# Two chunks of a depthwise convolution on ScalarE and GpSimd, one chunk fewer on TensorE, and the skip term on GpSimd

## The chip, the cores and the metric

The kernel runs on one core of one Trainium2 chip. Its time is the device time of one execution in microseconds (us), from the first to the last instruction on that core. A core has five engines that run side by side, each with its own queue in a fixed order: TensorE (PE), VectorE (DVE), ScalarE (ACT), GpSimd (POOL) and SyncE (SP, which here only issues DMAs). An instruction that waits holds up everything behind it on its own engine.

## The reference, cut to what matters

Two layers of a visual state-space block run one after the other over an image of 64 x 64 positions with 96 channels. In each layer an input projection gives 192 channels `x_val` and 192 gates `z`; `x_val` goes through a depthwise 3 x 3 convolution, a bias and SiLU. The result `u` feeds four selective scans, and the skip term `u * D` is added to their sum.

```python
xz = x @ in_proj_w                       # (H, W, 96) -> (H, W, 384)
x_val, z = (xz[..., :D_INNER], xz[..., D_INNER:])
xc = conv_general_dilated(xc, conv_w, (1, 1), 'SAME', feature_group_count=D_INNER) + conv_b
x_val = silu(xc)                         # u
y = scans(u) + u * D_skip                # four directions, summed
y = layernorm(y) * silu(z)
x = x + y @ out_proj_w
```

The convolution has nine taps; for each channel it is a sum of nine products of a shifted image with one weight of that channel.

## The kernel before, in words

`two_ss2d_layers` runs `head` (group norm, projections, convolution, gates), then the scans (`near_scans` in layer 0, `scans` in layer 1), then `tail`, once per layer. The change touches `head` alone, so it acts twice in an execution: at about 20 to 82 us (layer 0) and 205 to 271 us (layer 1).

The 192 channels lie as three blocks of 64 channels on 64 partitions; the two halves of each group of rows sit on partitions 0 to 63 and 64 to 127. A block has four chunks of 8 rows each per half, so a chunk is a tile of 128 partitions x 512 elements. Each block's projected image lies in SBUF with a border of zeros, `pad[b]` (128 x 4 chunks x 10 rows x 66 columns); `project` (line 1171) and `borders` (line 1183) fill it by TensorE and copies on ScalarE (lines 1179 and 1197).

There are two ways to convolve:

- `conv` (line 1237) runs on VectorE: one product with a weight (line 1251) and eight multiply-adds into an accumulator (line 1253). Over two chunks at once the operand is 2 x 526 = 1052 elements a partition, and both the image and the accumulator lie in SBUF. The accumulator comes from a pool with three buffers (tag `acc`).
- `conv_by_products` (line 1224) runs on TensorE: nine matmuls of one chunk with a diagonal matrix of the weights (line 1228), summed in PSUM.

Both end in `finish` (line 1217): ScalarE applies the bias and SiLU and writes `u` (line 1218), and `start_y` (line 1127) writes `y = D u` (line 1128), also on ScalarE.

The head's work, from line 1256 on: VectorE convolves block 0 (two pairs of chunks), block 1 (two pairs) and the last chunk of block 2; TensorE makes the first three chunks of block 2. The twelve gate chunks follow (`gate`, line 1201): a matmul (line 1205), SiLU on ScalarE (line 1210) and a DMA to HBM through three buffers (line 1211). The head isn't ordered by hand: the scheduler that records the program orders each engine's queue by its own estimates. On VectorE it lays two pairs of chunks into each other, a step of one and a step of the other by turns. The scans of layer 1 are in a hand-written order. GpSimd has almost nothing to do in the head: it clears the borders of `pad`.

After the head of layer 0, `near_scans` first copies parts of `u` by matmuls (`nu`, lines 283 to 299), in the order block 0, 1, 2. After the head of layer 1, `scans` first projects the last chunk of `u`, blocks 0, 1, 2 (`pj`, shown by the profile as line 675, since all its instructions are recorded by one helper).

Of the kernel before, what the change touches and what calls it, by code (L numbers as in the profile page):

```python
# [8 lines left out]
F32 = mybir.dt.float32  # L9
# [7 lines left out]
HW = 64  # L17
# [7 lines left out]
HT = TC // 2  # L25
NCH = L // TC
SR = HT // HW
# [9 lines left out]
V_CW, V_CB, V_G, V_B, V_D = 0, 9, 10, 11, 12  # L37
# [6 lines left out]
def two_ss2d_layers(  # L44
# [29 lines left out]
    nc = tc.nc  # L74
# [78 lines left out]
    with tc.tile_pool(name="ld", bufs=8) as ld, tc.tile_pool(  # L153
        name="ldp", bufs=4, space=PSUM
# [972 lines left out]
    def start_y(mul, ds, T, s=slice(0, L // 2)):  # L1127
        mul(y[T][:, s], u[T][:, s], ds[:, T : T + 1])

    def head(l, xT, w):  # L1130

        ipw_s, v, ds = w["ipw"], w["v"], w["ds"]
        with ExitStack() as sc:
            cv = sc.enter_context(tc.tile_pool(name=f"cv{l}", bufs=1))
            cw = sc.enter_context(tc.tile_pool(name=f"cw{l}", bufs=3))
            cvp = sc.enter_context(tc.tile_pool(name=f"cvp{l}", bufs=2, space=PSUM))

            pad = [cv.tile([128, NCH, SR + 2, HW + 2], F32, name=f"pad{l}_{b}") for b in range(3)]
# [24 lines left out]
            for g in range(8):  # L1163
                s = slice(g * 512, (g + 1) * 512)
# [6 lines left out]
            def project(b, c):  # L1171
                ps = cvp.tile([128, HT], F32, tag="in", name=f"in{l}_{b}_{c}", bufs=3)
                for h, half in enumerate(HALF):
                    g = 2 * c + h
                    nc.tensor.matmul(  # L1175
                        ps[half], ipw_s[:, 64 * b : 64 * b + 64], xn[:, g * 512 : (g + 1) * 512],
                        start=True, stop=True,
                    )
                nc.scalar.copy(
                    pad[b][:, c, 1 : SR + 1, 1 : HW + 1], ps.rearrange("p (r w) -> p r w", w=HW)  # L1180
                )

            def borders(b):

                ps = cvp.tile([128, 2, NCH, HW], F32, tag="ed", name=f"ed{l}_{b}")
                lhs = ipw_s[:, 64 * b : 64 * b + 64]
                for h, half in enumerate(HALF):
                    for below in range(2):

                        row = [SR * (2 * c + h + below) - 1 + below for c in range(NCH)]  # L1190
                        cs = [c for c in range(NCH) if 0 <= row[c] < HW]
                        s = slice(cs[0], cs[-1] + 1)
                        nc.tensor.matmul(
                            ps[half, below, s], lhs, xr[:, row[cs[0]] : row[cs[-1]] + 1 : 2 * SR],
                            start=True, stop=True,
                        )
                        nc.scalar.copy(
                            pad[b][half, s, (SR + 1) * below, 1 : HW + 1], ps[half, below, s]
                        )
# [13 lines left out]
            taps = [(i, j) for i in range(3) for j in range(3)]  # L1213

            W2 = HW + 2

            def finish(b, cut, of):
                nc.scalar.activation(
                    u[b][:, cut].rearrange("p (c r w) -> p c r w", r=SR, w=HW), of, AF.Silu,
                    bias=v[:, b, V_CB : V_CB + 1],  # L1220
                )
                start_y(nc.scalar.mul, ds, b, cut)

            def conv_by_products(b, c):

                ps = cvp.tile([128, HT], F32, tag="in", name=f"cp{l}_{b}_{c}", bufs=3)
                for k, (i, j) in enumerate(taps):
                    nc.tensor.matmul(  # L1228
                        ps.rearrange("p (r w) -> p r w", w=HW), diag[:, k, :],
                        pad[b][:, c, i : i + SR, j : j + HW],  # L1230
                        start=(k == 0), stop=(k == len(taps) - 1),
                    )
                finish(
                    b, slice(HT * c, HT * (c + 1)), ps.rearrange("p (c r w) -> p c r w", c=1, w=HW)
                )

            def conv(b, s):


                n = s.stop - s.start  # L1240
                room = cw.tile([128, 2, SR, W2], F32, tag="acc", name=f"acc{l}_{b}_{s.start}")
                room = room[:, 0:n]
                acc = room.rearrange("p c r w -> p c (r w)")[:, :, 0 : SR * W2 - 2]
                for k, (i, j) in enumerate(taps):
                    o = i * W2 + j
                    src = pad[b].rearrange("p c r w -> p c (r w)")[
                        :, s, o : o + SR * W2 - 2
                    ]
                    wk = v[:, b, V_CW + k : V_CW + k + 1]
                    if k == 0:  # L1250
                        nc.vector.tensor_scalar_mul(acc, src, wk)
                    else:
                        nc.vector.scalar_tensor_tensor(acc, src, wk, acc, ALU.mult, ALU.add)  # L1253
                finish(b, slice(HT * s.start, HT * s.stop), room[:, :, :, 0:HW])

            for b in (0, 1, 2):
                project(b, 0)
                project(b, 1)
                borders(b)
            for b in (2, 0, 1):  # L1260
                project(b, 2)
                project(b, 3)
            diag = cv.tile([128, len(taps), 128], F32, name=f"diag{l}")
            for k in range(len(taps)):
                nc.scalar.mul(diag[:, k, :], ident, v[:, 2, V_CW + k : V_CW + k + 1])
            conv(0, slice(0, 2))
            for c in range(NCH - 1):
                conv_by_products(2, c)
            for b, c in ((1, 0), (0, 2), (1, 2)):
                conv(b, slice(c, c + 2))  # L1270
            conv(2, slice(NCH - 1, NCH))
            for b in range(3):
                for c in range(NCH):
                    gate(b, c)
# [85 lines left out]
    for l in range(2):  # L1360

        w = {"st": st[l], "next": st[1]}
        ipw_s = w["ipw"] = wts.tile([DM, 2 * DI], F32, name=f"ipw{l}")
        nc.sync.dma_start(out=ipw_s, in_=ipw[l])
        v = w["v"] = wts.tile([128, 3, NV], F32, name=f"v{l}")
        op = w["op"] = wts.tile([128, 3, DM], F32, name=f"op{l}")
        for half in HALF:
            nc.sync.dma_start(out=v[half], in_=vec[l].rearrange("(b p) n -> p b n", b=3))
        for half in HALF:
            nc.sync.dma_start(out=op[half], in_=opw[l].rearrange("(b p) n -> p b n", b=3))  # L1370
        ds = w["ds"] = wts.tile([128, 3], F32, name=f"ds{l}")
        nc.vector.reduce_sum(ds, v[:, :, V_D : V_D + 4], axis=AX.X)
        sw = scan_weights(l)

        head(l, xT, w)
        xp.close()
        if l:
            scans(sw)
        else:
            covered = near_scans(sw)  # L1380
            with tc.If(covered < 1):
                for T in range(3):
                    start_y(nc.scalar.mul, ds, T)
                far_scans(sw)
        xp = ExitStack()
        xT = xp.enter_context(tc.tile_pool(name=f"xT{l + 1}", bufs=1)).tile(
            [DM, L], F32, name=f"xT{l + 1}"
        )
        tail(l, w, xT)
# [80 lines left out]
```

## Time and profile before

Times of three executions: 1526.31, 1535.46 and 1537.91 us, median 1535.46. The profiled execution is another one, with a span of 1528.7 us; that span is its own time, and every duration below is from it.

| stretch of the profiled execution | length | VectorE busy | ScalarE busy | TensorE busy | GpSimd busy |
|---|---|---|---|---|---|
| 30 to 80 us, convolution and gates of layer 0 | 50.0 | 48.5 | 29.0 | 45.9 | 0.0 |
| 80 to 125 us, start of the near scans | 45.0 | 27.6 | 28.7 | 15.2 | 18.2 |
| 221 to 271 us, convolution and gates of layer 1 | 50.0 | 49.1 | 28.8 | 45.9 | 0.0 |
| 300 to 1480 us, scans of layer 1 | 1180.0 | 1120.8 | 1036.3 | 987.1 | 1063.6 |

A line of the timeline gives the start in us from the start of the span, the time from the first start to the last end in us, the engine, the line of code, the operation, the output and inputs by tile name, the shape, and the number of instructions; in brackets how long the engine had stood idle before, and what ended that. A group's line gives busy us and mean ns of one.

### The profile page before, as it was taken

What the parts mean: (1) busy time and instruction counts of PE and PEld (TensorE: products, weight loads), DVE (VectorE), ACT (ScalarE), POOL (GpSimd) and SP (SyncE); (2) the same over time, 40 slices, a digit from 0 to 9 for tenths busy, and PEclk for the clock granted to TensorE, in tenths of its full rate; (3) what the DMA queues carried; (4) which work ended last, traced back from release to release, by engine and by line L of the source; (5) the groups of instructions that cost most, each with busy time, mean ns of one, the idle gap of its engine ahead of it and who ended that gap; (6) DMA issues with size and microseconds to landing.
All of it is one profiled execution on the core that took longest, in us unless ns stands there. A gap on an engine that the chain in (4) does not pass through costs nothing.

```text
span 1528.7 us, 17324 instructions
## 1 busy us (share of the span) xinstructions
PE 1238.4 (81%) x5122; PEld 499.9 (33%) x5122; DVE 1358.4 (89%) x946; ACT 1209.9 (79%) x2475; POOL 1103.3 (72%) x593
## 2 busy tenths in 40 slices
PE   6935779788887888888798889797888797877777
PEld 3323433333232333333332333333333232322223
DVE  5957579579999999999999999999999999999976
ACT  6554255679898989898998999989898998988733
POOL 0032000369899898989898989898999999898850
PEclk9965789589899999999999999999989999999999
DMA  4230511514352626262626262635344352626232
GB/s 111 79 85 2 134 44 69 140 29 111 85 130 65 148 61 153 55 140 56 140 57 138 57 144 70 142 75 127 91 104 109 87 128 68 150 59 152 55 105 75
DMA packets 79604, 146.33 MB, mean 96 GB/s; under 512 B 27484, under 2 KB 30748, under 8 KB 79404
## 3 DMA queue, kind: packets, MB, share of 16 engines
q1 hardware_dynamic: 78348, 142.78, 38.6%
q0 software_dynamic: 576, 1.57, 0.5%
q8 instruction: 42, 0.69, 0.2%
q10 hardware_dynamic: 576, 0.79, 0.2%
q14 instruction: 62, 0.51, 0.1%
HBM read 80.85 MB, written 12.13 MB: 61 GB/s over the span
## 4 chain that ended last, share of the span: by engine, by line
DVE 27%; issue 22%; PE 15%; ACT 10%; POOL 5%; DMA 5%; SPq 4%; DVEq 0%; ACTq 0%; POOLq 0%
DVE h L675 17%; DVE b L675 7%; PE ys L675 4%; ACT a L675 4%; SPq L675 4%; POOL hc L675 4%; PE b L675 3%; PE pj L675 3%; DMA cb<-C 2%; ACT bT L675 2%; PE pd L675 2%; PE cp L1228 2%; DMA szt<-szd 1%; DVE w L675 1%; PE in L1175 1%
## 5 line engine op out<-in xcount | busy, mean ns | idle before, releaser
L675 POOL TENSOR_TENSOR hc<-h,cb 128x1024 f32<-128x1024 f32 x384 | 903.3, 2369 | 115.1 <-DVE h L675 56.2
L675 DVE TENSOR_TENSOR_SCAN h<-a,carry,b 128x1024 f32<-128x1024 f32 x288 | 665.2, 2337 | 29.9 <-PE b L675 8.7
L675 ACT ACTIVATE a<-dt,am 128x1024 f32<-128x1024 f32 x384 | 438.8, 1143 | 93.5 <-DVE h L675 90.2
L675 PE MATMUL ys<-hc,fold 128*64 128x512 f32 x1536 | 431.9, 642 | 1.9 <-POOL hc L675 1.9
L675 ACT ACTIVATE bT<-duT,BT 128x192 f32<-128x192 f32 x1012 | 387.7, 446 | 9.9 <-PE b L675 8.0
L675 PE MATMUL b<-ident,bT 128*128 128x128 f32 x1536 | 219.5, 287 | 33.9 <-DVE h L675 28.3
L675 DVE TENSOR_TENSOR b<-b,du 128x1024 f32<-128x1024 f32 x192 | 232.2, 1209 | 12.4 <-PE b L675 12.4
L675 DVE TENSOR_TENSOR_SCAN h<-a,b 128x1024 f32<-128x1024 f32 x96 | 216.2, 2278 | 13.2 <-PE b L675 5.2
L675 PEld LDWEIGHTS b<-ident,bT 128*128 128x128 f32 x1536 | 174.1, 146 | 160.6 <-DVE h L675 98.9
L675 PE MATMUL b<-B,selh 96*128 96x512 bf16 x384 | 121.6, 400 | 92.2 <-DVE h L675 92.0
L675 PEld LDWEIGHTS ys<-hc,fold 128*64 128x64 f32 x1536 | 78.7, 139 | 140.4 <-issue 96.5
L675 PE MATMUL pj<-u,xw 64*124 64x512 f32 x192 | 98.4, 662 | 4.8 <-ACT sz L1210 3.5
L675 PE MATMUL pd<-xd,dwb 29*64 29x512 f32 x192 | 59.7, 698 | 52.3 <-DVE w L675 45.5
L675 PEld LDWEIGHTS <-selh 96*128 96x128 bf16 x384 | 25.9, 98 | 221.9 <-DVE h L675 123.8
L1253 DVE SCALAR_TENSOR_TENSOR acc<-pad,v,acc 128x1052 f32<-128x1052 f32 (+1 forms) x80 | 91.3, 1198 | 0.7
L675 POOL DMA_DIRECT2D du<-su x12 | 6.4, 538 | 80.4 <-ACT am L233 78.4
L675 PE MATMUL ys<-y,ident 128*128 128x512 f32 (+1 forms) x120 | 64.2, 643 | 0.0
L675 ACT CAST B<-pj 96x512 bf16<-96x512 f32 (+2 forms) x96 | 54.9, 575 | 4.4 <-PE pj L675 4.4
L675 POOL TENSOR_TENSOR sp<-sp,ln 128x512 f32<-128x512 f32 x45 | 57.6, 1279 | 0.2
L675 POOL TENSOR_TENSOR ln<-ln,w 128x512 f32<-128x512 f32 x45 | 57.6, 1280 | 0.0
L675 POOL TENSOR_TENSOR su<-sp,u 128x512 f32<-128x512 f32 x45 | 57.5, 1278 | 0.0
L675 PEld LDWEIGHTS pj<-u,xw 64*124 64x124 f32 x192 | 35.2, 198 | 65.0 <-issue 45.5
(175 smaller groups left out, 1185.1 us busy)
## 6 DMA issues: line engine op xcount, KB each, us to landing
cb<-C SPq DMA_DIRECT2D x256, 256.0 KB
dt<-sp SPq DMA_DIRECT2D x192, 128.0 KB
du<-su SPq DMA_DIRECT2D x180, 128.0 KB
szd<-sz SPq DMA_DIRECT2D x24, 256.0 KB
szt<-szd SPq DMA_DIRECT2D x24, 256.0 KB
xT<-xs SPq DMA_DIRECT2D x8, 384.0 KB
xs<-xT SPq DMA_DIRECT2D x1, 1536.0 KB
xs<-xT SPq DMA_DIRECT2D x8, 192.0 KB
```

Of the source, the lines that this page charges most:

```text
L675: return lambda *args, **more: tc.keep_in_program_order(op(*args, **more))
L1175: nc.tensor.matmul(ps[half], ipw_s[:, 64 * b : 64 * b + 64], xn[:, g * 512 : (g + 1) * 512], start=True, stop=True,)
L1228: nc.tensor.matmul(ps.rearrange("p (r w) -> p r w", w=HW), diag[:, k, :], pad[b][:, c, i : i + SR, j : j + HW], start=(k == 0), stop=(k == ...
L1253: nc.vector.scalar_tensor_tensor(acc, src, wk, acc, ALU.mult, ALU.add)
```

## The change

Four edits, all in `head`:

1. A new function `conv_by_two` convolves two chunks without VectorE. ScalarE makes nine products of the shifted image with a weight (the first into the accumulator, the others into one of two buffers, tag `tap`), and GpSimd adds the eight others to the accumulator one after the other. It is called for chunks 2 and 3 of block 1.
2. TensorE convolves two chunks of block 2 instead of three, and VectorE the last two instead of the last one. VectorE thus has four pairs of chunks, and no single chunk.
3. `y = D u` is written by GpSimd, not ScalarE.
4. Chunks 2 and 3 of the blocks are projected in the order 1, 0, 2, not 2, 0, 1.

```diff
-                start_y(nc.scalar.mul, ds, b, cut)
+                start_y(nc.gpsimd.tensor_scalar_mul, ds, b, cut)
...
+            def conv_by_two(b, s):
+
+                n = s.stop - s.start
+                room = cw.tile([128, 2, SR, W2], F32, tag="accp", name=f"acc{l}_{b}_{s.start}", bufs=1)
+                room = room[:, 0:n]
+                acc = room.rearrange("p c r w -> p c (r w)")[:, :, 0 : SR * W2 - 2]
+                for k, (i, j) in enumerate(taps):
+                    o = i * W2 + j
+                    src = pad[b].rearrange("p c r w -> p c (r w)")[
+                        :, s, o : o + SR * W2 - 2
+                    ]
+                    wk = v[:, b, V_CW + k : V_CW + k + 1]
+                    if k == 0:
+                        nc.scalar.mul(acc, src, wk)
+                        continue
+                    part = cw.tile(
+                        [128, 2, SR, W2], F32, tag="tap", name=f"tap{l}_{b}_{s.start}_{k}", bufs=2
+                    )[:, 0:n].rearrange("p c r w -> p c (r w)")[:, :, 0 : SR * W2 - 2]
+                    nc.scalar.mul(part, src, wk)
+                    nc.gpsimd.tensor_add(acc, acc, part)
+                finish(b, slice(HT * s.start, HT * s.stop), room[:, :, :, 0:HW])
...
-            for b in (2, 0, 1):
+            for b in (1, 0, 2):
                 project(b, 2)
                 project(b, 3)
...
             conv(0, slice(0, 2))
-            for c in range(NCH - 1):
+            conv_by_two(1, slice(2, NCH))
+            for c in range(NCH - 2):
                 conv_by_products(2, c)
-            for b, c in ((1, 0), (0, 2), (1, 2)):
-                conv(b, slice(c, c + 2))
-            conv(2, slice(NCH - 1, NCH))
+            for b, s in ((1, slice(0, 2)), (0, slice(2, NCH)), (2, slice(2, NCH))):
+                conv(b, s)
```

## The prediction

> **What bounds the kernel now.** First the page, for the span and what GpSimd's operations cost:
>
> ```profile
> span 1528.7 us, 17324 instructions
> ...
> L675 POOL TENSOR_TENSOR hc<-h,cb 128x1024 f32<-128x1024 f32 x384 | 903.3, 2369 | 115.1 <-DVE h L675 56.2
> ...
> L675 POOL TENSOR_TENSOR su<-sp,u 128x512 f32<-128x512 f32 x45 | 57.5, 1278 | 0.0
> ```
>
> Two-input GpSimd operations cost 2369 ns at 1024 elements and 1278 at 512: 2.13 ns an element plus 0.19 us. Then VectorE's timeline over the convolution of layer 0:
>
> ```profile
> 29.96 0.77 DVE L1251 TENSOR_SCALAR acc<-pad,v 128x1052 f32<-128x1052 f32 x1 [7.60 <-ACT pad L1197]
> ...
> 32.68 17.23 DVE L1253 SCALAR_TENSOR_TENSOR acc<-pad,v,acc 128x1052 f32<-128x1052 f32 x14
> 49.83 0.76 DVE L1251 TENSOR_SCALAR acc<-pad,v 128x1052 f32<-128x1052 f32 x1
> ...
> 52.95 0.76 DVE L1251 TENSOR_SCALAR acc<-pad,v 128x1052 f32<-128x1052 f32 x1
> 53.63 17.23 DVE L1253 SCALAR_TENSOR_TENSOR acc<-pad,v,acc 128x1052 f32<-128x1052 f32 x14
> 70.78 0.49 DVE L1251 TENSOR_SCALAR acc<-pad,v 128x526 f32<-128x526 f32 x1
> ...
> 73.21 5.65 DVE L1253 SCALAR_TENSOR_TENSOR acc<-pad,v,acc 128x526 f32<-128x526 f32 x7
> ```
>
> No idle time from 29.96 to 78.86: VectorE sets the length of this stage, 48.9 us, and again in layer 1 (221.25 to 270.14). A multiply-add of a pair takes 17.23 / 14 = 1.23 us, its product 0.68, a pair 0.68 + 8 x 1.23 = 10.5; the single chunk 0.41 + 8 x 0.81 = 6.9. What follows waits a little earlier, in layer 1 on TensorE's timeline:
>
> ```profile
> 268.43 8.07 PE L675 MATMUL pj<-u,xw 64*124 64x512 f32 x12 [3.49 <-ACT sz L1210]
> ```
>
> `pj` starts 1.7 us before VectorE ends, when the last gate leaves ScalarE; block 2 is needed only by its third matmul. In layer 0 the copies `nu` likewise run from 76.90 to 84.75, block 2 last.
>
> Last, do VectorE and GpSimd disturb each other? In the convolution GpSimd is idle, so I look where both work, at the start of the near scans; GpSimd first, then VectorE:
>
> ```profile
> 95.94 1.23 POOL L335 CAST nB<-nleft 32x768 bf16<-32x768 f32 x1
> 101.33 3.77 POOL L370 TENSOR_TENSOR ndu<-nv,nus 64x1152 f32<-64x1152 f32 x1 [4.16 <-DVE nv L361]
> ```
>
> ```profile
> 96.60 1.79 DVE L359 TENSOR_TENSOR nw<-nw,nt 128x1152 f32<-128x1152 f32 x1
> ...
> 99.89 1.36 DVE L361 TENSOR_TENSOR nv<-nv,nln 128x1152 f32<-128x1152 f32 x1
> 101.29 1.35 DVE L370 TENSOR_TENSOR ndu<-nv,nus 64x1152 f32<-64x1152 f32 x1
> 102.67 4.85 DVE L372 TENSOR_TENSOR_SCAN nsums<-steady,nv 128x1152 f32<-128x1152 f32 x1
> ```
>
> They take turns. L359 takes 1.79 us and L361, of the same form, 1.36: L359 ends 1.22 us after GpSimd's cast does (97.17). GpSimd's L370 should take 0.19 + 1152 x 2.13 = 2.64 and takes 3.77: it ends (105.10) 2.46 after VectorE's L370 (102.64). The scan L372, some 2.6 us by the shorter scans, takes 4.85: it ends (107.52) 2.42 after GpSimd's L370. All three VectorE operations have two inputs in SBUF.
>
> **What the Trainium skill says.** "SBUF — State Buffer", section "Who interferes with whom": a VectorE instruction with two SBUF inputs shares a read path with a GpSimd instruction that reads SBUF, and the one that comes second "fully blocks" until the other ends; so does a VectorE operation with one source in a two-port mode. The three pairs above agree. It also says one SBUF input on VectorE does no harm: in the scans, where `b` lies in PSUM, GpSimd's products keep to 2369 ns. "GPSIMD Engine Reference", section "Engine selection": one-input GpSimd operations run roughly at line rate, two-input ones about twice as slow as on VectorE. The trace has the second (2369 ns against 1.36 us at 1152); for the first, a cast of 768 elements takes 0.82 us, 0.82 ns an element beside a fixed 0.19.
>
> **The change part by part**, in layer 0 (layer 1 has the same order on every engine).
>
> *Removed from VectorE:* the single chunk, 6.9. Its four pairs are 42.0 us: alone they would end at 72.0, not 78.86.
>
> *Added on GpSimd:* eight additions of 1052 elements, 0.19 + 1052 x 2.13 = 2.43 us each, 19.4 in all. Each reads two tiles of SBUF while VectorE runs multiply-adds, which read two tiles of SBUF (`pad`, `acc`). By the turns above each addition stops VectorE for as long as it holds the path: between 2.25 (2.43 less the 0.18 by which 2.46 falls short of 2.64, spent before it needs the path) and 2.43. I take 2.3: 8 x 2.3 = 18.4. If the lock did not hold here it would be 0, the lower bound (additions elsewhere can't make a multiply-add shorter); against 0 speak only the three pairs.
>
> *Who wins the path hardly matters.* By turns, an addition and a multiply-add take 3.45 us together; the first starts at 41.3 (its operand comes from ScalarE at 40.1), the eighth ends at 67.8. If VectorE always won, the additions would run later, when VectorE waits for a buffer (below), at the same total.
>
> *Added on ScalarE:* nine products of about 1.17 us (row `y<-u,ds`, 1.15 at 1024), 10.5, minus seven or eight `y` writes, 7.4. With two `tap` buffers product k waits for addition k-2, so ScalarE's queue stands in the taps until addition 6 ends (60.9). Behind it stand the SiLU table load, `u` of block 1, then `u` of chunks 0 and 1 of block 0, which frees the `acc` buffer VectorE's fourth pair needs; then the gates. By turns: addition 8 at 67.8, `u` 69.0, buffer free at 70.2; VectorE reaches that pair at 72.4, because it was held up itself. No stall, slack 2.2. The gates run from 72.4 to about 85 (before, twelve took 13.2 with interruptions), free some 6 us before VectorE's last `u`. Hence nothing on the path. Their twelve DMAs on SP's queue move with them, by about 9 us; SP's next work, the rows `nC` of the near scans (before, at 88.08) or `C` of the scans, comes after VectorE's end and moves further. If VectorE ended before 86, the gates would set the end instead.
>
> *TensorE:* nine matmuls fewer, 23.45 / 3 = 7.8 us, hidden: TensorE then waits for gates, and VectorE ends later.
>
> *`y` on GpSimd:* sizes 512, 1024, 1024, 1024, 512 fall while VectorE still convolves. No row has this operation on long tiles. Low: line rate, 0.43 and 0.85 of the path, 3.4 in all; high: 1.9 cycles an element at 1.2 GHz ("GPSIMD Engine Reference", "Performance pitfalls for Q7 kernels", an estimate), 6.5. I take 3.9, near the cast's rate. Two more `y` writes come as VectorE ends; `pj` and `nu` don't wait for them, nor does the memset behind them, needed 6 us later.
>
> *Order of projections:* block 1 first costs nothing; the first pairs need chunks 0 and 1 only.
>
> *What follows:* the last SiLU is 1.15 instead of 0.72. But block 0's last pair ends 2.5 us before block 2's. Layer 0: after `u` of block 2 (VectorE's end + 1.25) only that block's last `nu` matmuls remain, 2.1 us: + 3.4, before + 5.9, gain 2.5. Layer 1: `pj` begins when `u` of block 0 is there, 1.3 before VectorE's end instead of 1.7: loss 0.4.
>
> *Sum:* VectorE ends at 78.86 - 6.9 + 18.4 + 3.9 = 94.3, i.e. + 15.4. Layer 0: + 15.4 - 2.5 = + 12.9; layer 1: + 15.4 + 0.4 = + 15.8. Together + 28.7: 1528.7 becomes 1557.4. The median of the runs lies 6.8 above the span, so **1564 us**, 1.9% slower. The case's own range: 17.4 to 19.4 for the additions, 3.4 to 6.5 for `y`, 2 us a layer for handing over: + 24 to + 42, 1555 to 1582 beside noise of some 5 each way.
>
> **The rivals.** *No lock, but the buffer (same).* VectorE isn't held up and reaches the fourth pair at 52.95. Additions of 2.49 with their gaps end at 60.1, the buffer comes at 62.4: VectorE stalls 9.5 us and ends at 81.7, + 2.9. Layers + 0.4 and + 3.3: 1539. For: no trace shows this very multiply-add beside GpSimd. Against: the two other forms with two SBUF inputs were both held.
>
> *Faster.* Neither lock nor stall: VectorE ends at 72.0, layers - 9.3 and - 6.4: 1520. This needs, besides no lock, the eighth addition before 50.7, so additions under 1.3 us each; the row says 2.4. Almost excluded.
>
> *Slower still.* One-input `y` at the high price, and VectorE waiting also for the buffer, if additions come late: 5 to 10 us a layer more, 1575 to 1585.
>
> **How the numbers follow.** Lock as worked out 0.75 (1555 to 1575), slower still 0.15, no lock 0.08, faster 0.02. Range 1547 to 1583. Within 1% (about what a measurement of this kernel tells from no change, 1520 to 1551) lies the second case; slower by over 1% lie the first and third: 0.90.
>
> **What would show it.** Right: multiply-adds while GpSimd adds show about 3.5 us instead of 1.31, eight in each layer; VectorE ends near 94 in layer 0; additions show more than 2.43, since they wait too. Wrong: 1.31 throughout and a gap of VectorE ahead of the fourth pair, ended by ScalarE, would be the second case; a gap besides the long multiply-adds the third.

## The result, and the profile after

The changed kernel takes 1569.06 us (median of four executions, 1563.4 to 1574.8) against 1535.55 of the kernel before (four, 1526.31 to 1537.91): a ratio of 1.0244, 95% interval 1.0215 to 1.0272. (The ratios here and below are those on record; they aren't the quotients of the printed medians.) It is slower, and the time lies 5 us from the 1564 predicted. The way there is not the one predicted as likeliest.

From the page of the changed kernel, the span and the rows of the new additions and of VectorE's multiply-adds (busy us and mean ns; idle time before, and what ended it):

```profile
span 1570.4 us, 17283 instructions
...
L1256 POOL TENSOR_TENSOR acc<-acc,tap 128x1052 f32<-128x1052 f32 x16 | 64.1, 4008 | 47.0 <-ACT tap L1255 45.9
...
L1275 DVE SCALAR_TENSOR_TENSOR acc<-pad,v,acc 128x1052 f32<-128x1052 f32 x64 | 83.6, 1375 | 0.1
```

An addition takes 4008 ns in the mean where 2430 were worked out; a multiply-add 1375, hardly more than the 1.31 us of one that nothing holds up. The mean hides the shape of it. All additions of the changed kernel by their line (min, median and max duration in ns):

```profile
L1256 POOL TENSOR_TENSOR acc<-acc,tap x16: 2402/2408/15221, 41.7 to 280.6; 128x1052 f32<-128x1052 f32 x16
```

Sixteen additions, eight a layer: the median is 2408, and one of 15.2 us makes the mean. VectorE's, GpSimd's and ScalarE's timelines in layer 0 say which one:

```profile
34.30 17.24 DVE L1275 SCALAR_TENSOR_TENSOR acc<-pad,v,acc 128x1052 f32<-128x1052 f32 x14
51.45 0.77 DVE L1273 TENSOR_SCALAR acc<-pad,v 128x1052 f32<-128x1052 f32 x1
52.13 2.54 DVE L1275 SCALAR_TENSOR_TENSOR acc<-pad,v,acc 128x1052 f32<-128x1052 f32 x2
76.65 0.87 DVE L1273 TENSOR_SCALAR acc<-pad,v 128x1052 f32<-128x1052 f32 x1 [21.99 <-ACT u L1218]
77.44 19.45 DVE L1275 SCALAR_TENSOR_TENSOR acc<-pad,v,acc 128x1052 f32<-128x1052 f32 x14
```

```profile
41.72 32.61 POOL L1256 TENSOR_TENSOR acc<-acc,tap 128x1052 f32<-128x1052 f32 x8 [23.00 <-ACT tap L1255]
74.30 12.56 POOL L1128 TENSOR_SCALAR y<-u,ds 128x512 f32<-128x512 f32 x5
```

```profile
41.93 1.18 ACT L1255 ACTIVATE tap<-pad,v 128x1052 f32<-128x1052 f32 x1
56.96 1.17 ACT L1255 ACTIVATE tap<-pad,v 128x1052 f32<-128x1052 f32 x1 [13.85 <-POOL acc L1256]
...
74.36 3.23 ACT L1218 ACTIVATE u<-acc,v 128x1024 f32<-128x1024 f32 x3 [1.80 <-POOL acc L1256]
```

GpSimd's first addition starts at 41.72 and gets nowhere until VectorE stops at 54.67: 41.72 + 15.22 = 56.94. VectorE's fourteen multiply-adds before that take 17.24 us, as before (17.23). They alternate between the accumulators of two pairs, start every 1.23 us and take 1.31, so each starts 0.08 us before the last has ended. The product at 51.45, which has only one input that is a tile, is laid into this chain in the same way (it starts 0.09 before the last has ended) and doesn't let the addition in either. ScalarE stands in the taps behind the addition (13.85 us), so `u` of block 0, which frees VectorE's third accumulator, comes only at 75.5 to 76.6; VectorE, whose fourth pair needs it, stands 21.99 us, and in that time the eight additions run. The `y` behind them come later than that and are still not kept out: GpSimd is at work when VectorE starts again at 76.65, and the five take 12.56 us in a row (11.7 by their medians, below), while fourteen multiply-adds take 19.45 us instead of 17.24. Layer 1 is the same, 21.99 again.

In what follows I compare heads. Head 0 runs from VectorE's first product of the convolution to ScalarE's copy into `nxd`; head 1 from the first product to VectorE's first `wl` of the scans. All starts are read from the timelines.

| kernel (its label below) | VectorE, first product to last multiply-add, layer 0 | head 0 | head 1 | both, against before | span |
|---|---|---|---|---|---|
| before | 48.90 | 57.03 | 60.58 | | 1528.7 |
| changed | 66.65 | 73.47 | 77.10 | +33.0 | 1570.4 |
| acc4 | 44.27 | 86.51 | 90.45 | +59.4 | 1588.3 |
| gaps4 | 65.12 | 72.92 | 77.29 | +32.6 | 1560.3 |
| no_sums | 42.98 | 58.80 | 55.11 | -3.7 | 1529.8 |
| no_sums_ys | 42.25 | 47.66 | 53.45 | -16.5 | 1512.4 |
| y_scalar | 64.32 | 72.06 | 78.09 | +32.5 | 1565.9 |
| y_gpsimd_only | 50.67 | 62.14 | 62.36 | +6.9 | 1539.5 |
| psum_before | 68.06 | 78.38 | 80.52 | +41.3 | 1573.1 |
| psum_acc | 60.34 | 72.15 | 73.24 | +27.8 | 1564.8 |
| gates_between | 48.90 | 53.87 | 60.59 | -3.2 | 1526.0 |
| relief_gates | 47.39 | 53.55 | 58.93 | -5.1 | 1530.7 |
| mixed_gates | 45.44 | 55.52 | 54.32 | -7.8 | 1528.2 |
| mixed_gates_fs | 51.30 | 57.90 | 63.63 | +3.9 | 1526.8 |

The span less both heads is 1411.1 us before and 1419.8 after, and 1405.3 to 1419.8 over these fourteen profiles. So of the 41.7 us between the two profiles 33.0 are the heads, which is also about the difference of the medians (33.5); the other 8.7 can't be told from what one execution differs from the next.

### The profile page after: what moved, and what is told of

It is laid out like the page before. It is cut to its first block, busy times and chain, and to the rows that moved or that the text cites. A ratio compares the mean times of both kernels' runs of the same rounds, so it can differ in the third digit from the quotient of the medians.

```text
span 1570.4 us, 17283 instructions
## 1 busy us (share of the span) xinstructions
PE 1233.6 (79%) x5086; PEld 494.5 (31%) x5086; DVE 1350.9 (86%) x928; ACT 1216.1 (77%) x2475; POOL 1206.8 (77%) x623
## 3 DMA queue, kind: packets, MB, share of 16 engines
q0 software_dynamic: 576, 1.57, 0.4%
## 4 chain that ended last, share of the span: by engine, by line
DVE 28%; issue 21%; PE 15%; ACT 11%; POOL 5%; DMA 4%; SPq 4%; DVEq 0%; ACTq 0%; POOLq 0%
DVE h L675 16%; DVE b L675 7%; PE ys L675 5%; ACT a L675 4%; SPq L675 4%; PE b L675 3%; PE pj L675 3%; ACT bT L675 2%; DMA cb<-C 2%; POOL acc L1256 2%; POOL hc L675 2%; PE pd L675 2%; DVE acc L1275 1%; DVE w L675 1%; DMA dt<-sp 1%
## 5 line engine op out<-in xcount | busy, mean ns | idle before, releaser
L1256 POOL TENSOR_TENSOR acc<-acc,tap 128x1052 f32<-128x1052 f32 x16 | 64.1, 4008 | 47.0 <-ACT tap L1255 45.9
L1275 DVE SCALAR_TENSOR_TENSOR acc<-pad,v,acc 128x1052 f32<-128x1052 f32 x64 | 83.6, 1375 | 0.1
L1205 PE MATMUL z<-xn,ipw 96*64 96x512 f32 x96 | 27.9, 690 | 40.2 <-ACT sz L1210 40.2
```

The costliest lines, as they stand in the source:

```text
L1205: nc.tensor.matmul(ps[half], ipw_s[:, DI + 64 * b : DI + 64 * b + 64], xn[:, g * 512 : (g + 1) * 512], start=True, stop=True,)
L1256: nc.gpsimd.tensor_add(acc, acc, part)
```

## The experiments

Theory A, formed on the trace after: a chain of VectorE instructions with two inputs in SBUF, each starting before the last has ended, keeps a waiting GpSimd instruction out for as long as it lasts. Theory B, the prediction's: the engines take turns. Theory C: no shared path, only the buffer. Each ratio below is against further executions of the kernel before, with medians of 1530.9 to 1531.81 us.

**acc4**: four accumulators, so that VectorE never waits for one.

```diff
-                room = cw.tile([128, 2, SR, W2], F32, tag="acc", name=f"acc{l}_{b}_{s.start}")
+                room = cw.tile([128, 2, SR, W2], F32, tag="acc", name=f"acc{l}_{b}_{s.start}", bufs=4)
```

> The changed kernel with four acc buffers on VectorE instead of three, so that its fourth pair waits for no buffer. Theory A (a chain of two-input VectorE instructions with no gap between them keeps GpSimd out of SBUF for as long as it lasts): multiply-adds stay at 1.31 us, VectorE runs from 31.6 to about 73.6 in layer 0 without a stall; the first addition waits until then, some 31 us, and the eight end near 94 (73.6 + 8 x 2.49). ScalarE, behind them, then has four u and twelve gates left and ends its part near 107 instead of 99.4: each head some 7 to 9 us longer than with the change, profiled span near 1586. Theory B (the two engines take turns): multiply-adds beside an addition 3.5 us, VectorE ends near 94 to 96, additions end near 70, heads 3 to 5 us shorter, span near 1562. Theory C (no shared path, only the buffer): additions of 2.4 us from 41.7 to 62, VectorE ends near 74, gates near 84, heads 15 us shorter, span near 1540.

Measured: 1591.18 us, ratio 1.0421 (1.0368 to 1.0474). VectorE's timeline at the end of its chain, and the additions by their line:

```profile
55.62 17.23 DVE L1275 SCALAR_TENSOR_TENSOR acc<-pad,v,acc 128x1052 f32<-128x1052 f32 x14
72.77 0.16 DVE L1394 TENSOR_REDUCE ds<-v 128x3 f32<-128x12 f32 x1
72.89 3.33 DVE L1275 SCALAR_TENSOR_TENSOR acc<-pad,v,acc 128x1052 f32<-128x1052 f32 x1
```

```profile
L1256 POOL TENSOR_TENSOR acc<-acc,tap x16: 2402/2405/33047, 42.1 to 313.4; 128x1052 f32<-128x1052 f32 x16
```

With the stall gone the kernel is slower still, by 26.4 us in the heads: the first addition now lasts 33.0 us instead of 15.2. Less the 2.4 us that it takes alone, it gets in near 72.7, at the end of the last multiply-add but one; the one left then waits for it, 3.33 us. VectorE runs a reduction of 0.16 us there (72.77), but that isn't what lets the addition in: in layer 1 the chain holds no reduction, and the first addition ends its wait at the same place (it starts at 264.54, lasts 33.05 and so gets in near 295.2). VectorE there:

```profile
294.02 1.30 DVE L1275 SCALAR_TENSOR_TENSOR acc<-pad,v,acc 128x1052 f32<-128x1052 f32 x1
295.37 3.33 DVE L1275 SCALAR_TENSOR_TENSOR acc<-pad,v,acc 128x1052 f32<-128x1052 f32 x1
```

These are the last two steps of the fourth pair. The third pair is done, so for the first time since the addition came two multiply-adds in a row go into one accumulator, and the second starts about 0.04 us after the first has ended, not 0.08 before. Nothing else of VectorE's lies there, so the gap is what is left to let the addition in; no run changes it alone. This place also says what makes the chain unbroken: two pairs laid into each other. B and C are out: a free buffer should have helped under both.

**gaps4**: acc4, and after every multiply-add VectorE clears one unused element.

```diff
                         nc.vector.scalar_tensor_tensor(acc, src, wk, acc, ALU.mult, ALU.add)
+                        nc.vector.memset(room[:, 0, 0, HW : HW + 1], 0.0)
```

> As acc4, and after every multiply-add VectorE overwrites one unused element of its accumulator (a memset of one element per partition, in a padding column that nothing uses), so that every one to three multiply-adds VectorE leaves SBUF's read path alone for some 0.06 us; 32 such in a layer, 2 us. Theory A (only a chain without a gap keeps GpSimd out): GpSimd gets in at the first gap, near 42 us; from there an addition and one or two multiply-adds by turns, eight multiply-adds of about 3.5 us, VectorE ends near 73.6 + 2 + 18.4 = 94, or 96 with y; additions end near 72; span about 1564, some 20 us below acc4. Theory A' (VectorE has priority whenever both want the path, gap or not): no addition before VectorE ends near 76, span as acc4 plus 4. Theory B (turns anyway): no difference to acc4 but the 2 us of memsets in each layer. Theory C: 1.31 us throughout, span near 1544.

Measured: 1564.27 us, ratio 1.0226 (1.0188 to 1.0264). VectorE's timeline between 45 and 52 us, then the additions:

```profile
45.15 3.45 DVE L1275 SCALAR_TENSOR_TENSOR acc<-pad,v,acc 128x1052 f32<-128x1052 f32 x1
45.17 0.06 DVE L1276 MEMSET acc<- 128x1 f32 x1
48.52 3.46 DVE L1275 SCALAR_TENSOR_TENSOR acc<-pad,v,acc 128x1052 f32<-128x1052 f32 x1
```

```profile
L1256 POOL TENSOR_TENSOR acc<-acc,tap x16: 3292/3302/3357, 40.8 to 273.5; 128x1052 f32<-128x1052 f32 x16
```

More work on VectorE, and 27 us faster than acc4 (28.0 between the spans). A memset of 0.06 us between multiply-adds is enough: no addition waits longer than one multiply-add (3302 - 2408 = 0.9 us), and a multiply-add beside one takes 3.45 us. This is the prediction's picture, by turns, with its number; it is just not what an unbroken chain did. It also ends where the changed kernel ends: the heads are 0.4 us apart.

**no_sums** and **no_sums_ys**: the additions left out, with `y` on GpSimd and on ScalarE.

```diff
-                    nc.gpsimd.tensor_add(acc, acc, part)
```

```diff
-                start_y(nc.gpsimd.tensor_scalar_mul, ds, b, cut)
+                start_y(nc.scalar.mul, ds, b, cut)
```

> The changed kernel without its eight additions on GpSimd: eight of the nine taps of block 1's last two chunks are computed and not added, so the output is incomplete; the products and everything else stay. It shows what the additions cost in all. Every theory: ScalarE isn't held in the taps, so the u that frees VectorE's buffer comes in time, VectorE runs from 31.6 to about 73.6 without a stall of more than 1 us and ends some 22 to 25 us earlier in each layer. Theory A: y waits as well while VectorE's chain has no gap, so the seven y run mostly after 73.6, to about 91 (2 of 1.57 us and 5 of 2.84), and GpSimd's memsets for the near scans come at 92 instead of 82: heads 15 to 20 us shorter than with the change, span 1530 to 1540. Theories B and C: y runs in between (B: VectorE ends near 78), heads 20 to 22 us shorter, span about 1527.

> The changed kernel without its eight additions (eight of nine taps of block 1's last two chunks are left out) and with y back on ScalarE: GpSimd has nothing to do in the convolution. All theories: VectorE runs its 42.0 us without a stall and ends near 71 to 73, the heads are 9 and 6 us shorter than in the kernel before, span about 1513. Against the run without additions that kept y on GpSimd (1529.8) this says what GpSimd's y costs where the additions aren't in its way: theory A 9 us in layer 0 (ScalarE's copy into nxd no longer waits for GpSimd's memset) and about 5 in layer 1.

Measured: 1526.86 us, ratio 0.9977 (0.9964 to 0.9991), and 1515.99 us, ratio 0.9910 (0.9882 to 0.9939). VectorE runs through, 42.98 and 42.25 us. The rest is `y`. GpSimd and ScalarE in no_sums:

```profile
50.18 37.45 POOL L1128 TENSOR_SCALAR y<-u,ds 128x1024 f32<-128x1024 f32 x7 [32.74 <-issue]
87.69 0.73 POOL L270 MEMSET nxd<- 32x768 f32 x1
```

```profile
88.45 0.48 ACT L312 COPY nxd<-npj 124x384 f32<-124x384 f32 x1 [11.09 <-POOL nxd L270]
```

The first `y` starts at 50.18 and is let in near 70.4, again ahead of the last multiply-add of the chain, so the seven run to 87.6; the memset of `nxd` stands behind them, and ScalarE waits 11.09 us for it. With `y` back on ScalarE both heads together are 12.8 us shorter, and 16.5 shorter than before. That is what there would be to win if the work taken from VectorE cost nothing on GpSimd (the prediction's "faster" had 15.7).

**y_gpsimd_only**: the kernel before with the first line of the change alone.

```diff
-                start_y(nc.scalar.mul, ds, b, cut)
+                start_y(nc.gpsimd.tensor_scalar_mul, ds, b, cut)
```

> The kernel before with y = D u on GpSimd and nothing else changed. Theory A: VectorE's chain has no gap from 30 to 78.9, so no y runs before it ends: the eight y (four of 2.84, four of 1.57 us) run from 78.9 to about 97, GpSimd's memset of nxd behind them comes at 97 instead of 81.5, and ScalarE's copy into nxd, which was at 87.0, waits for it until 98: + 11 us in layer 0. In layer 1 the du transfers behind y on GpSimd come some 2 us later. VectorE's multiply-adds keep to 1.31. Span about 1542. Theory B (turns): y of 2.8 and 1.6 us by turns with VectorE, which ends 10 us or so later with multiply-adds of over 3 us, no late memset: + 20 us over both layers. The prediction's price (line rate, by turns): + 4 a layer, 1537. Theory C (no shared path): no change, 1529.

Measured: 1541.61 us, ratio 1.0063 (1.0044 to 1.0082). ScalarE's copy into `nxd`, and GpSimd's `y` by their line:

```profile
93.38 0.48 ACT L312 COPY nxd<-npj 124x384 f32<-124x384 f32 x1 [7.91 <-POOL nxd L270]
```

```profile
L1128 POOL TENSOR_SCALAR y<-u,ds x16: 1561/2844/26851, 49.0 to 289.4; 128x512 f32<-128x512 f32 x8, 128x1024 f32<-128x1024 f32 x8
```

Again the first is kept waiting (it lasts 26.9 us). An operation with one input waits like an addition. Head 0 is 5.1 us longer, where 11 were expected: the first `y` is let in near 74.3, and from then on the `y` keep coming, though seven multiply-adds are still to run; those take 7.43 us instead of 5.65. VectorE's timeline, the seven together, then the first three of them:

```profile
74.36 0.16 DVE L1372 TENSOR_REDUCE ds<-v 128x3 f32<-128x12 f32 x1
74.48 7.43 DVE L1253 SCALAR_TENSOR_TENSOR acc<-pad,v,acc 128x526 f32<-128x526 f32 x7
```

```profile
74.48 1.08 DVE L1253 SCALAR_TENSOR_TENSOR acc<-pad,v,acc 128x526 f32<-128x526 f32 x1
75.60 2.30 DVE L1253 SCALAR_TENSOR_TENSOR acc<-pad,v,acc 128x526 f32<-128x526 f32 x2
```

The seven belong to the single chunk, all in one accumulator, and start about 0.04 us after the last has ended (74.48 + 1.08 = 75.56, then 75.60). So here the chain ended where its two accumulators became one, as in acc4. The changed kernel does call for an amendment of theory A: after its stall two pairs are laid into each other again, each multiply-add starts 0.08 us before the last has ended, and the `y` get in nonetheless. There GpSimd was at work when the chain began; once it is in, it gets its turns, gap or not.

**y_scalar**: the changed kernel with `y` back on ScalarE (the second diff above).

> The changed kernel with y = D u back on ScalarE. Theory A: GpSimd's y took the path while VectorE stood or late in the chain, and cost VectorE the 2.2 us by which its last fourteen multiply-adds are longer (19.45 instead of 17.24): 2.2 us a layer come back; the stall of 22 us stays, since ScalarE's y for block 1 come behind the u that frees the buffer. Span 1570.4 - 4 = 1566. Theory of the prediction (3.9 us a layer at line rate): 1562.6. If y on ScalarE stands ahead of that u after all, the stall grows by up to 2.3 us a layer and the span stays at 1570.

Measured: 1568.57 us, ratio 1.0248 (1.0205 to 1.0292), no different from the changed kernel. VectorE does end 2.3 us earlier after its stall (17.23 us for fourteen multiply-adds, not 19.45), but what follows takes longer by 0.9 in layer 0 and 3.1 in layer 1, since ScalarE now has `y` between its last `u`: the heads differ by 0.4 us. Beside the additions `y` is worth nothing either way.

**psum_acc** and its control **psum_before**: VectorE's accumulators in PSUM, in the changed kernel and in the one before. Each multiply-add then takes one chunk of 512 elements, and projections and gates get fewer PSUM buffers to make room.

```diff
-                room = cw.tile([128, 2, SR, W2], F32, tag="acc", name=f"acc{l}_{b}_{s.start}")
+                room = cvp.tile([128, 2, HT], F32, tag="accv", name=f"acc{l}_{b}_{s.start}", bufs=2)
...
+                    for c in range(n):
+                        acc = room[:, c].rearrange("p (r w) -> p r w", w=HW)
+                        src = pad[b][:, s.start + c, i : i + SR, j : j + HW]
...
```

> The changed kernel with VectorE's accumulators in PSUM (two of 128x2x512, multiply-adds chunk by chunk on 512 elements, and fewer banks for projections and gates), so that a multiply-add reads one operand from SBUF and one from PSUM. To be set against the same edit of the kernel before. Theory A (the path is SBUF's, and only two SBUF inputs hold it): the eight additions run at 2.4 us each from about 42 to 62 while VectorE works, and VectorE's multiply-adds beside them are no longer than those alone. Theory D (a long VectorE chain keeps GpSimd out wherever its operands lie): the first addition waits for a gap of VectorE, over 10 us, as with the change. In time: 64 multiply-adds of 0.8 to 0.9 us make some 56 us of VectorE, its end near 88 to 96 by how long its third pair waits for a bank; span 1555 to 1575. It need not be faster; what counts is the additions' wait and the difference to its control: under A some 5 us a layer faster than the control (nine chunks on VectorE there, eight here, less y), under D slower than it.

> The kernel before with VectorE's accumulators in PSUM, as the control for the run before: nine chunks of nine instructions of 0.8 to 0.9 us, some 66 to 72 us of VectorE instead of 48.9, so 17 to 23 us a layer more: span 1560 to 1575.

Measured: 1562.44 us, ratio 1.0191 (1.0147 to 1.0235), and 1575.64, ratio 1.0294 (1.0254 to 1.0333). VectorE in psum_acc while GpSimd adds, the same stretch of psum_before, and the additions of psum_acc:

```profile
38.92 12.73 DVE L1271 SCALAR_TENSOR_TENSOR acc<-pad,v,acc 128x512 f32<-128x512 f32 x19
```

```profile
39.72 12.73 DVE L1249 SCALAR_TENSOR_TENSOR acc<-pad,v,acc 128x512 f32<-128x512 f32 x19
```

```profile
L1256 POOL TENSOR_TENSOR acc<-acc,tap x16: 2408/2418/2432, 43.4 to 268.9; 128x1052 f32<-128x1052 f32 x16
```

Not one addition waits, and VectorE's chain is as long as in the control, though it has no gap either where the first of them start. So it is SBUF that they share, and a multiply-add with one input in SBUF and its accumulator in PSUM does no harm; whether its read or its write decides isn't separated. The split of the work then pays: 13.5 us in the heads against its control. Both lose against the kernel before by 128x512 instructions (one every 0.67 us, 1.34 for a pair; from SBUF 1.23) and by stalls for PSUM banks (9.6 us in psum_acc).

Last, I tried what these runs suggest for a faster kernel. **gates_between** puts three gates ahead of each of TensorE's chunks; **relief_gates** adds that ScalarE writes the first product of VectorE's later accumulators, of which there are five; **mixed_gates** instead gives the single chunk to ScalarE and GpSimd, beside a pair of VectorE that accumulates in PSUM; **mixed_gates_fs** does both, with four accumulators. The `conv_by_two` of the last two isn't that of the change: ScalarE makes eight products of one chunk, each into a buffer of its own, GpSimd does seven additions, and VectorE adds the ninth tap (`last`). GpSimd has no `y` in any of them. All start from the kernel before.

```diff
             for c in range(NCH - 1):
+                for b in range(3):
+                    gate(b, c)
                 conv_by_products(2, c)
+            for b in range(3):
+                gate(b, NCH - 1)
...
```

```diff
-                        nc.vector.tensor_scalar_mul(acc, src, wk)
+                        mul = nc.vector.tensor_scalar_mul if (b, s.start) == (0, 0) else nc.scalar.mul
+                        mul(acc, src, wk)
```

```diff
-            for b, c in ((1, 0), (0, 2), (1, 2)):
-                conv(b, slice(c, c + 2))
-            conv(2, slice(NCH - 1, NCH))
...
+            conv(1, slice(0, 2))
+            last = conv_by_two(2, NCH - 1)
+            conv_in_psum(0, slice(2, NCH))
+            conv(1, slice(2, NCH))
+            last()
```

> The kernel before with the twelve gates placed between TensorE's chunks instead of after them: three gates ahead of each of the three chunks and three at the end, so that ScalarE does nine of them in time in which it was idle (46.9 to 62 us). A control for the next ones. VectorE's 48.9 us stay; in layer 0 the copies nu of blocks 0 and 1 no longer wait for the last gate and may start 2 to 3 us earlier, layer 1 stays bound by VectorE's end. Span 1528.7 - 3 = 1526, at most 5 less; 1529 if nothing waits for the gates.

> As the run with the gates between, and ScalarE instead of VectorE writes the product of the first tap for all accumulators but the first (five accumulators, so that it needn't wait): VectorE loses three products of 0.68 and one of 0.41 us, 2.45 a layer, GpSimd does nothing. Span 1526 - 5 = 1521. If a product comes late from ScalarE's queue, VectorE shows a gap ahead of a pair and the gain is gone.

> The single chunk leaves VectorE in a way that theory A allows. ScalarE writes eight of its nine products (526 elements, a buffer for each, so that it never waits), GpSimd adds them up (seven additions of about 1.3 us), VectorE does the ninth tap (0.81 us) late; and the pair of VectorE that runs at that time (chunks 2 and 3 of block 0) accumulates in PSUM, eighteen instructions of 0.66 us, so that GpSimd has SBUF's read path for 12 us. y stays on ScalarE, gates lie between TensorE's chunks. Theory A: the first addition waits until VectorE reaches the PSUM pair near 51, the seven are done near 61, no VectorE instruction is held up; VectorE takes 3 x 10.5 + 11.9 + 0.8 = 44.2 instead of 48.9 us; span 1526 - 9 = 1517. Theory D (VectorE's chain keeps GpSimd out wherever its operands lie) is out by the run with all accumulators in PSUM; if it held, additions would wait until about 72 and the span would be 1530.

> Both: the single chunk by ScalarE and GpSimd beside a PSUM pair, gates between, and the first product of VectorE's second and fourth pair by ScalarE (four accumulators). VectorE 44.2 - 1.4 = 42.8 us; span 1517 - 3 = 1514, if ScalarE's and TensorE's parts (TensorE ends near 73) don't set the end instead: then about 1516.

Measured: 1528.50 us, ratio 0.9968 (0.9951 to 0.9986); 1527.71, 0.9966 (0.9953 to 0.9980); 1530.49, 0.9989 (0.9973 to 1.0004); 1537.51, 1.0031 (1.0013 to 1.0050). The first two beat both kernels, by 0.3% against the one before; the gain is nearly all the gates', 3.2 us in head 0. The first product on ScalarE comes late once (a gap of 0.84 us on VectorE), and its 1.5 us a layer don't show in the time.

The additions of mixed_gates and VectorE's chain while the first one waits:

```profile
L1294 POOL TENSOR_TENSOR acp<-acp,tap x14: 1298/1305/11562, 40.2 to 251.0; 128x526 f32<-128x526 f32 x14
```

```profile
32.69 0.76 DVE L1251 TENSOR_SCALAR acc<-pad,v 128x1052 f32<-128x1052 f32 x1
33.37 17.23 DVE L1253 SCALAR_TENSOR_TENSOR acc<-pad,v,acc 128x1052 f32<-128x1052 f32 x14
```

The same of mixed_gates_fs:

```profile
L1295 POOL TENSOR_TENSOR acp<-acp,tap x14: 2026/2192/2200, 40.8 to 249.2; 128x526 f32<-128x526 f32 x14
```

```profile
34.22 22.30 DVE L1254 SCALAR_TENSOR_TENSOR acc<-pad,v,acc 128x1052 f32<-128x1052 f32 x13 [0.84 <-ACT acc L1252]
```

In mixed_gates it went as theory A has it: the first addition lasts 11.6 us, until VectorE comes to the PSUM pair, of the other six one takes 2.2 and five 1.3, and VectorE's part is 45.4 us. The heads are 7.8 us shorter, yet the time is hardly, and a span of 1517 was expected: its profile shows 7.3 us more outside the heads (1418.4). That isn't one odd execution, for the profiled one (1530.03) lies at the median of 22. In its trace the gain is still there after 150 of the 384 `hc` operations of layer 1 and is gone after 250; what took it stays open.

In mixed_gates_fs theory A fails. There the additions are let in from 40.8 us on, each after one multiply-add, by turns, although VectorE's multiply-adds have no gap then and are those of mixed_gates; the chain lengthens by 6.3 us, and the span of 1514 that was expected was missed by 12.8 in the profiled execution, one of the two fastest of 22. Turns once begun go on, that is the amendment; but what let the first one in stays open. Four things differ from mixed_gates: the chain holds no product of VectorE (in mixed_gates the one at 32.69 lies in it), VectorE had waited 0.84 us for a product of ScalarE some six us earlier, the buffers lie elsewhere, and the addition came at another moment of a multiply-add. Of these the moment is the least likely: a first GpSimd operation was kept out when it came 0.07 us (changed kernel, acc4), 0.39 us (y_gpsimd_only) and 0.72 us (mixed_gates) into a multiply-add, and let in at 0.44. Which of them decides was not tried.

## Why the prediction came out right, and where it was wrong

*The removed chunk, -6.9.* Right. With nothing on GpSimd, VectorE needs 42.25 us for its four pairs; 42.0 was worked out.

*Eight additions, by turns, +18.4.* The failed step. VectorE's chain doesn't give way at all, so the multiply-adds stay at 1.31 and the mark named for "right" (3.5 us, eight a layer) is absent. I took the turns from three pairs at the near scans, where each VectorE instruction starts only after the last has ended; in the convolution they start every 1.23 us and take 1.31. The trace of before showed both, and I didn't ask whether the difference matters. The gap of acc4 and the memsets of gaps4 show that it does; mixed_gates_fs shows that it isn't the whole rule.

*"Who wins the path hardly matters."* Right, and it is what saved the number: if VectorE always won, the additions would run later, while VectorE waits for a buffer. They do: 19.7 us from VectorE's stop at 54.67 to the last addition's end at 74.33, then two `u` of 1.15, together the stall of 21.99. The term is 22.0 instead of 18.4. gaps4, which does take turns, has heads of the same length to 0.4 us. But it holds only as long as there is such a wait; acc4 took it away and lost 26.4 us more. The number came out right by this sentence, not by the mechanism that it was summed from.

*"No stall", slack 2.2 us.* Wrong, a consequence of the same step: ScalarE stands in the taps until 69.4 instead of 60.9. The 72.4 in that passage also takes the additions at 19.4, not at the 18.4 of the sum; with 18.4 the slack would have been 1.2.

*`y` on GpSimd, +3.9.* Mis-sized in both directions. It takes 2.84 us at 1024 elements and 1.57 at 512, three times the rate assumed and more than the high price too (11.7 for five against 6.5), but costs VectorE less than that: the five ran partly in the stall, partly beside the last pairs, and lengthened those by 2.2 us (19.45 against 17.24). "Nor does the memset behind them, needed 6 us later" held here only because VectorE's stall gave `y` its time; in y_gpsimd_only it was waited for, 7.9 us.

*VectorE ends + 15.4.* It is + 17.75 in the stage (48.90 to 66.65): -6.65 for the chunk (42.25 against 48.90), + 21.99, + 2.2, and 0.2 at a product.

*What follows: gain 2.5 in layer 0, loss 0.4 in layer 1.* Measured from VectorE's end to the end of the heads: gains of 1.3 and 1.1. Sum: + 16.4 and + 16.5 instead of + 12.9 and + 15.8; + 33.0 instead of + 28.7. (The range stated, + 24 to + 42, is some 2 us wider at each end than its own terms give, about + 26 to + 40.)

*The rivals.* "No lock, but the buffer" was given 0.08 and the sign "1.31 throughout and a gap ahead of the fourth pair, ended by ScalarE". Exactly that sign appeared, with the lock in force: the sign was shared by two causes, since a GpSimd kept out entirely leaves VectorE undisturbed too. The length of the gap (9.5 us without a lock, 22.0 measured) and an addition's longest duration (15.2 us) tell them apart. "Faster" needed no lock; no_sums_ys shows what it would have brought.

*What the Trainium skill says.* "SBUF — State Buffer", section "Who interferes with whom", is borne out in its main point and in a finer one: outside the two-port modes, a VectorE instruction with one SBUF input does no harm (2418 ns beside VectorE's multiply-adds into PSUM in psum_acc). It gives the shared pair to whoever issues first "for the whole instruction". Here it stayed with VectorE over a whole chain of instructions, up to 30.6 us; in gaps4 and mixed_gates_fs it changed hands at every instruction. "GPSIMD Engine Reference", section "Engine selection", has one-input operations roughly at line rate; a product with a per-partition scalar takes 2.84 us for 1024 elements here, more than an addition of two tiles (2.37, row `hc`).

## What to carry to other kernels

Before moving work to GpSimd, look at what VectorE runs at that time: if it is an unbroken chain with two operands in SBUF, GpSimd may get nothing done until the chain breaks for a moment, and then what counts is who is queued behind GpSimd. Two accumulators used by turns make such a chain; two steps in a row into one accumulator leave a gap of some 0.04 us, and there GpSimd got in. (Ordering VectorE's pairs one after the other for that purpose was not tried.) Longest durations show the wait, medians don't. Where such a chain can't be avoided, VectorE's accumulator can go to PSUM for that time, as in psum_acc, or the work can stay on ScalarE, as `y` does in no_sums_ys; one more buffer only prolonged the wait here.

## What was not expected of the hardware

- One VectorE instruction of 0.06 us (a memset of one element) between multiply-adds changed GpSimd's longest wait from 30.6 us (33.05 - 2.41) to 0.9, and the kernel by 28 us.
- Where two multiply-adds in a row go into one accumulator, the second starts some 0.04 us after the first has ended, and in acc4, no_sums and y_gpsimd_only that is where a GpSimd operation that had waited 20 to 31 us got in, in both layers.
- An unbroken chain kept GpSimd out in six kernels and let it in by turns in one (mixed_gates_fs, both layers); the traces don't show by what.
- Multiply-adds into PSUM follow each other every 0.67 us for 512 elements, 1.34 for the two chunks of a pair; into SBUF every 1.23 us for 1052, 1024 of them useful.
- A product with a per-partition scalar on GpSimd takes 2.84 us for 1024 elements.
